# A four-layer sequence model on one core: the FP4 network rewritten as a pipeline of half batches, its quantizing of weights and inputs moved into the first attention, the second attention begun inside it

## The chip, the cores and the metric

The kernel runs on one core of one Trainium2 chip, as one launch. The metric is the device time in microseconds (us). A core has a matrix engine (PE, with its weight loads listed as PEld), a vector engine (DVE), a scalar engine (ACT), a general engine (POOL) and a queue engine that only issues transfers (SP). Each engine takes its own list of instructions strictly in order, and waits on semaphores for the others.

## The reference

The input is `x`, 8 batches of 512 tokens of width 128, fp32. Four blocks follow each other, each as `x = layernorm(x + block(x))`:

```
attention 0:  16 heads of width 8, softmax(q k^T / sqrt(8) - slope * |i-j|) v, output projection
FP4 network:  h = silu(xq @ gate_q^T) * (xq @ up_q^T);  y = hq @ down_q^T      (inner width 352)
attention 1:  16 heads of width 8, plain softmax, output projection
local block:  2 layers of local attention (8 heads of 64, window 64) and a gated network
```

The index `q` in the FP4 network is a quantization of blocks of 16 neighbours in the last dimension: the scale is max|block| / 6, each element divided by the scale is rounded to the nearest of 0, 0.5, 1, 1.5, 2, 3, 4, 6 with its sign, and multiplied by the scale again. It is applied to the input `x`, to the three weights and to the hidden `h`.

## The kernel before

The state lives in SBUF for the whole program: `xn` (the normalised activations) and `xs` (the sums), each 128 partitions x 32 token tiles x 128. `body` runs `attention(0, ...)`, clears some rows of `ks_`, then `ffn0`, `attention(1, ...)` and `ffn1`.

**attention.** A batch has 4 groups of 4 heads, and a group is a unit of 8 steps; 8 batches give 256 steps. A step (function `step`, from line 212) does for unit n the matrix products of scores `s_ps` (query rows against keys) and their row maximum `m` on DVE (L239), and for the unit two before (16 steps, `LAG`) the transposed scores `t_ps` with the maximum already folded in, and the exponentials `e` on ACT (L245). `values` multiplies `e` with `va` on PE. At fixed steps other work is hung in through the table `todo`: `shift` (transposes the maxima and sends them by a POOL transfer into a row of `q`, L257), `divide` (L282, L284), `end_o` and `end_y` at the end of a batch, and the operands of the next batch: `begin_x`, `begin_qk` (which splits q and k into two parts on POOL, L167 and L168, and writes them to DRAM), `load_qk` (which reads them back as `q` and `k`, L184) and `begin_v`. `end_y` ends in `add_and_stats` (L94 to L99 on DVE) and `layernorm` (L104, L105, L116 on POOL). PE's instructions are kept in the written order (L126, L127); the order on DVE, ACT and POOL is made when the program is built, by a scheduler that places an instruction where it expects its inputs to be ready. `p_s` holds two score tiles, `p_t` three banks, `e` thirteen tiles.

**Batch 0 of each attention** has its operands made ahead of the first step, with nothing beside them.

**ffn0.** `quantized` (L374 to L384) is ten instructions: a blockwise maximum, three small ones for the scale and its inverse on DVE, a product on POOL (L379), four on DVE (L380 to L383, the first takes the exponent bits of each element), a product on POOL (L384). The three weights are loaded and quantized at its start, turned by PE and copied by ACT. Then for each of 8 batches: `begin` quantizes the input (512 columns), `gated` turns it, does the gate and up products for 4 token tiles, `silu` and the product (L426, L427), and quantizes `h` for each half batch (704 columns); `down` turns the result, multiplies with `wd`, and adds (L94 to L99), and `layernorm` ends on ACT (L112). Nothing here is held in the written order.

Of the kernel before, what the change touches and what calls it, by code (L numbers as in the profile page):

```python
# [9 lines left out]
F32 = mybir.dt.float32  # L10
# [8 lines left out]
P = 128  # L19
B, S, D = 8, 512, 128  # L20
NT = S // P
# [19 lines left out]
def body(ctx, tc, x, consts, rows, wa0, wa1, acols, bo, wf, wqkv, wo, w1, w2, cols, b2r, qs, ks, out):  # L41
# [77 lines left out]


    def attention(li, alibi, qs_, ks_, late=None):
# [6 lines left out]
        with ExitStack() as st:  # L128
# [11 lines left out]
            qb = const.tile([P, 1], F32, name="qb")  # L140
            nc.vector.tensor_tensor(qb, col[:, 0:1], col[:, 1:2], ALU.mult)
            va = []
            for i in range(2):
                v = const.tile([P, NT, 16, 32], F32, name=f"va{i}")
                nc.gpsimd.memset(v, 0.0)
                nc.gpsimd.memset(v[:, :, :, 8:9], 1.0)
                va.append(v)


            def begin_x(b, h):  # L150
                ps = bank("xt_ps")
                for c in range(NT):
                    tr(ps[:, c * P : (c + 1) * P], xn[:, b * NT + c, :], ident)
                h["xT"] = work.tile([P, S], F32, tag="xT", name="xT", bufs=1)
                nc.scalar.copy(h["xT"], ps)

            def begin_qk(b, h, n):
                ps = bank("qk_ps")
                mm(ps, lhsT=w[:, n * P : (n + 1) * P], rhs=h["xT"], start=True, stop=True)
                t = work.tile([P, S], F32, tag=f"x{n}", name="x", bufs=1)  # L160
                if n == 0:
                    nc.scalar.activation(t, ps, AF.Identity, bias=qb, scale=col[:, 0:1])  # L162
                else:
                    nc.scalar.activation(t, ps, AF.Identity, bias=col[:, 2:3])
                parts = work.tile([P, 2, S], F32R, tag=f"hl{n}", name="parts", bufs=1)
                hi, lo = parts[:, 0, :], parts[:, 1, :]
                nc.gpsimd.tensor_copy(hi, t)  # L167
                nc.gpsimd.tensor_tensor(lo, t, hi.bitcast(F32), ALU.subtract)  # L168

                far = dram.tile([2, 2, 64, S], F32R, tag=f"far{n}", name="far")  # L170
                for j in range(2):
                    nc.sync.dma_start(
                        out=far[j].bitcast(F32).rearrange("a c t -> c a t"), in_=parts[64 * j : 64 * j + 64].bitcast(F32)
                    )
                h["far", n] = far

            def load_qk(b, h, n, part):

                dst, pp = (qs_, ks_)[n][b % 2], slice(4 * part, 4 * part + 4)
                for j in range(2):  # L180
                    both = h["far", n][j].bitcast(F32).rearrange("a (p d) t -> a d p t", d=8)
                    for r in range(4):
                        at = 64 * j + 8 * r
                        nc.sync.dma_start(  # L184
                            out=dst[at : at + 8, pp].bitcast(F32), in_=both[r // 2 if n == 0 else r % 2][:, pp]
                        )

            def begin_v(b, h):
                h["o"] = work.tile([P, NT, P], F32, tag="o", name="o", bufs=3)
                ps = bank("v_ps").rearrange("p (c d) -> p c d", c=NT)  # L190
                for c in range(NT):
                    mm(ps[:, c, :], lhsT=h["xT"][:, c * P : (c + 1) * P], rhs=w[:, W_V : W_V + P], start=True, stop=True)
                nc.scalar.copy(va[b % 2][:, :, :, 0:8], ps.rearrange("p c (h d) -> p c h d", d=8))
# [15 lines left out]
            def step(u, i, v, k):  # L209
# [30 lines left out]
                if v:  # L240
                    if alibi:
                        corrected(ts, vlo, 64, True)
                    for j in range(2):
                        e = work.tile([P, S], F32, tag="e", name="e", bufs=13)
                        nc.scalar.activation(e, ts[j], AF.Exp, scale=float(SLOPES[2 * vp + j]) if alibi else 1.0)  # L245
                        v["e"].append(e)
# [64 lines left out]
            batch, units = [{} for _ in range(B)], []  # L311
            for n in range(B * G):
# [8 lines left out]
                if g == 0 and b + 1 < B:  # L321
# [9 lines left out]
                    later(s + 20, with_bias, b + 1)  # L331
                if g == G - 1:
                    later(z + 15, end_o, batch[b])
                    later(z + 18, end_y, b, batch[b])

            begin_x(0, batch[0])
            begin_qk(0, batch[0], 0)
            begin_qk(0, batch[0], 1)
            for part in range(2):
                for j in range(2):  # L340
                    load_qk(0, batch[0], j, part)
            begin_v(0, batch[0])
# [3 lines left out]
            with_bias(0)  # L346
            if late:
                late()
            for s in range(B * G * NU + LAG + 20):
# [8 lines left out]
    def ffn0():  # L358
        with ExitStack() as st:
            pool = lambda name, bufs, **k: st.enter_context(tc.tile_pool(name=f"f{name}", bufs=bufs, **k))  # L360
            const, work = pool("c", 1), pool("w", 2)
            p_g, p_t = pool("g", 2, space=PSUM), pool("t", 4, space=PSUM)

            def quantized(src, n, tag):

                nb = n // 16
                blocks = lambda t: t.rearrange("p (n k) -> p n k", k=16)  # L370
                over = lambda t: t.unsqueeze(2).broadcast_to([P, nb, 16])
                tile_ = lambda name, w: work.tile([P, w], F32, tag=f"{name}{tag}", name=name)
                sc, inv, y, m = tile_("sc", nb), tile_("inv", nb), tile_("y", n), tile_("m", n)
                nc.vector.tensor_reduce(sc, blocks(src), AX.X, ALU.max, apply_absolute_value=True)  # L374
                nc.vector.tensor_scalar(sc, sc, float(np.float32(1.0) / np.float32(6.0)), 1e-12, ALU.mult, ALU.max)
                nc.vector.reciprocal(inv, sc)

                nc.vector.tensor_scalar_mul(inv, inv, 1.0 - 2.0**-23)
                nc.gpsimd.tensor_tensor(blocks(y), blocks(src), over(inv), ALU.mult)  # L379
                nc.vector.tensor_single_scalar(m.bitcast(I32), y.bitcast(I32), 0x7F800000, ALU.bitwise_and)  # L380
                nc.vector.tensor_scalar(m, m, 1.0, 1.5 * 2.0**22, ALU.max, ALU.mult)
                nc.vector.tensor_tensor(y, y, m, ALU.add)
                nc.vector.tensor_tensor(y, y, m, ALU.subtract)  # L383
                nc.gpsimd.tensor_tensor(blocks(y), blocks(y), over(sc), ALU.mult)  # L384
                return y


            wgu = const.tile([P, 2, NI], F32, name="wgu")
            wd = const.tile([P, 3, D], F32, name="wd")
            wraw = const.tile([P, F_ALL], F32, name="wraw")  # L390
            nc.sync.dma_start(out=wraw, in_=wf)
            for j in range(2):
                wq = quantized(wraw[:, j * 3 * P : (j + 1) * 3 * P], 3 * P, "w")
                ps = p_t.tile([P, 3 * P], F32, tag="tr", name="w_ps")
                for c in range(3):
                    nc.tensor.transpose(ps[:, c * P : (c + 1) * P], wq[:, c * P : (c + 1) * P], ident)
                nc.scalar.copy(wgu[:, j, :], ps[:, 0:NI])
            wq = quantized(wraw[:, 6 * P : F_ALL], NI, "w")
            ps = p_t.tile([P, 3, P], F32, tag="tr", name="wd_ps")
            for c, (at, n) in enumerate(I_CH):  # L400
                nc.tensor.transpose(ps[0:n, c, :], wq[:, at : at + n], ident)
            for c, (at, n) in enumerate(I_CH):
                nc.scalar.copy(wd[0:n, c, :], ps[0:n, c, :])

            def begin(b):
                return quantized(xn[:, b * NT : (b + 1) * NT, :].rearrange("p c d -> p (c d)"), S, "x")

            def gated(b, xq):
                ps = p_t.tile([P, S], F32, tag="tr", name="xq_ps")
                for c in range(NT):  # L410
                    nc.tensor.transpose(ps[:, c * P : (c + 1) * P], xq[:, c * P : (c + 1) * P], ident)
                xqT = work.tile([P, S], F32, tag="xqT", name="xqT")
                nc.scalar.copy(xqT, ps)
                hq = []
                for half in range(2):
# [15 lines left out]
            def down(b, hq):  # L431
                for half in range(2):
                    hT = work.tile([P, 3, 2, P], F32, tag="hT", name="hT")
                    for c, (at, n) in enumerate(I_CH):
                        ps = p_t.tile([P, 2, P], F32, tag="tr", name="hq_ps")
                        for t in range(2):
                            nc.tensor.transpose(ps[0:n, t, :], hq[half][:, t * NI + at : t * NI + at + n], ident)
# [478 lines left out]
```

## Time and profile before

| what | us |
|---|---|
| median of 3 runs (2046.76 to 2053.12) | 2050.5 |
| the profiled execution, its device time | 2052.7 |
| its span, first to last instruction | 2050.9 |
| first row maximum of attention 0 | 39.1 |
| last `xn` of attention 0 normalised (L116) | 535.3 |
| last `xn` of the FP4 network normalised (L112) | 723.9 |
| first row maximum of attention 1 | 746.5 |
| 17th row maximum of attention 1 (first step with exponentials) | 766.8 |

The times of the last five rows are counted from the start of the span. The page gives busy shares of the engines, in the span (PE 83%, DVE 71%, ACT 57%, POOL 40%) and in 40 slices of 51 us, with the clock that the matrix engine was granted. Attention 0 fills slices 2 to 11, the FP4 network 11 to 15, attention 1 15 to 23, the local block the rest. A row of groups reads: line, engine, operation, result<-inputs, shapes, count | busy us, mean ns of one | idle time of the engine just before, and what ended it.

### The profile page before, as it was taken

Reading aid. Unit: us, or ns where it says so; the run is one execution under the profiler, and the core shown is the slowest. Engines: PE = TensorE matmul, PEld = TensorE weight load, DVE = VectorE, ACT = ScalarE, POOL = GpSimd, SP = SyncE. Lnnn points to the kernel's source line nnn. Section 1 sums busy time; section 2 is a strip of 40 time slices with the busy share of each in tenths; the row PEclk is TensorE's granted clock in tenths of the full one; section 3 lists DMA queues with packets and bytes.
Section 4 is the critical chain, followed back from the end, with each engine's and each line's share of the span. In section 5 each row is a group of like instructions: output and inputs, shape, how many; then the busy total and the mean of one; then the engine's idle time right before and its main releaser. Section 6 shows DMA issues by size and latency. Waiting matters only on the chain.

```text
span 2050.9 us, 41924 instructions
## 1 busy us (share of the span) xinstructions
PE 1712.4 (83%) x16277; PEld 981.8 (48%) x16293; DVE 1459.0 (71%) x2612; ACT 1168.8 (57%) x2749; POOL 829.0 (40%) x880
## 2 busy tenths in 40 slices
PE   1899999999476559999999757888988888888893
PEld 0445455555254424444444324556556555656562
DVE  2677777776588648888889356777777777777752
ACT  0376777777232217877778515566665566655650
POOL 3402222213445451222221434555555555666653
PEclk6699999999787659999999869999999999999997
DMA  5722222310000033333320001111111111111110
GB/s 115 185 54 64 62 52 57 64 23 2 12 1 0 0 97 79 66 65 64 71 63 2 22 16 24 30 31 33 30 32 34 33 32 32 35 35 32 29 30 21
DMA packets 91640, 88.68 MB, mean 43 GB/s; under 512 B 45825, under 2 KB 57473, under 8 KB 91442
## 3 DMA queue, kind: packets, MB, share of 16 engines
q1 hardware_dynamic: 86752, 85.00, 19.1%
q8 instruction: 129, 2.11, 0.4%
q0 software_dynamic: 4096, 0.54, 0.2%
q14 instruction: 69, 0.57, 0.1%
q10 hardware_dynamic: 594, 0.47, 0.1%
HBM read 41.33 MB, written 18.87 MB: 29 GB/s over the span
## 4 chain that ended last, share of the span: by engine, by line
PE 23%; DVE 19%; ACT 15%; POOL 3%; issue 2%; DMA 1%; SPq 1%; ACTq 0%; POOLq 0%; DVEq 0%
ACT pw L466 8%; PE av L126 6%; PE s_ps L126 5%; DVE t L567 4%; DVE r L563 4%; DVE ss L571 3%; PE t_ps L126 3%; DVE m L627 3%; ACT sq L466 2%; PE qk_ps L464 2%; ACT e L245 1%; DVE nrm L590 1%; PE qk_ps L126 1%; DVE u L742 1%; PE p_ps L465 1%
## 5 line engine op out<-in xcount | busy, mean ns | idle before, releaser
L239 DVE TENSOR_REDUCE m<-s_ps 128x2 f32<-128x1024 f32 x512 | 624.2, 1225 | 207.1 <-PE s_ps L126 203.0
L245 ACT ACTIVATE e<-t_ps 128x512 f32<-128x512 f32 x1024 | 555.8, 595 | 185.4 <-PE t_ps L126 175.2
L126 PE MATMUL av<-e,va 128*32 128x256 f32 x4096 | 328.6, 393 | 10.4 <-ACT avs L274 10.3
L466 ACT ACTIVATE pw<-sp,m,nrm 128x128 f32<-128x128 f32 x512 | 226.5, 461 | 183.7 <-DVE m L629 183.0
L126 PE MATMUL s_ps<-k,q 63*128 63x512 f32 x1024 | 266.9, 515 | 48.3 <-DMA k<-far 24.0
L126 PE MATMUL t_ps<-q,k 64*128 64x512 f32 x1024 | 249.0, 449 | 0.0
L257 POOL DMA_DIRECT2D q<-mt x128 | 68.4, 538 | 437.7 <-ACT mt L253 437.7
L126 PEld LDWEIGHTS s_ps<-k,q 63*128 63x128 f32 x1024 | 100.3, 190 | 242.2 <-issue 153.9
L640 POOL TENSOR_TENSOR pw<-pw,den 128x1024 f32<-128x1024 f32 x64 | 121.2, 1894 | 211.3 <-DVE den L639 169.1
L574 POOL TENSOR_TENSOR r<-r,t 128x1024 f32<-128x1024 f32 x64 | 151.0, 2359 | 97.5 <-DVE t L567 95.1
L563 DVE TENSOR_TENSOR r<-qk_ps,tab 128x512 f32<-128x512 f32 x128 | 87.3, 682 | 103.0 <-ACT sq L466 103.0
L464 PE MATMUL qk_ps<-wqkv_s,hT 128*128 128x512 f32 x256 | 136.3, 659 | 16.7 <-DVE t L567 15.9
L126 PEld LDWEIGHTS t_ps<-q,k 64*128 64x128 f32 x1024 | 122.9, 189 | 20.7 <-ACT e L245 10.6
L126 PEld LDWEIGHTS av<-e,va 128*32 128x32 f32 x4096 | 81.8, 108 | 104.1 <-issue 68.8
L465 PE MATMUL p_ps<-cst,pw 128*128 128x128 f32 x512 | 76.3, 284 | 55.1 <-DVE xs L705 31.1
L466 ACT ACTIVATION_READ_ACCUMULATOR pw<-sp,m,nrm 128x1 f32 x512 | 106.1, 207 | 0.0
L126 PEld LDWEIGHTS <-sel 64*128 64x128 bf16 x2048 | 66.8, 97 | 76.4 <-issue 46.6
L467 ACT COPY v<-v_ps 128x512 f32<-128x512 f32 x64 | 37.6, 587 | 105.5 <-PE v_ps L464 105.5
L567 DVE TENSOR_TENSOR t<-qk_ps,tab 128x256 f32<-128x256 f32 x256 | 95.4, 414 | 0.0
L671 DVE COPY pT<-p_ps 128x512 f32<-128x512 f32 x128 | 84.2, 686 | 15.3 <-PE p_ps L465 14.6
L465 PEld LDWEIGHTS p_ps<-cst,pw 128*128 128x128 f32 x512 | 55.8, 142 | 72.3 <-DVE xs L705 25.3
L167 POOL CAST parts<-x 128x512 fp32r<-128x512 f32 x32 | 19.4, 607 | 170.3 <-ACT x L162 166.4
(161 smaller groups left out, 3234.3 us busy)
## 6 DMA issues: line engine op xcount, KB each, us to landing
far<-parts SPq DMA_DIRECT2D x64, 256.0 KB
q<-far SPq DMA_DIRECT2D x256, 64.0 KB
k<-far SPq DMA_DIRECT2D x256, 64.0 KB
ve<-v SPq DMA_DIRECT2D x112, 128.0 KB
xn<-in_x SPq DMA_DIRECT2D x8, 256.0 KB
q<-mt POOLq DMA_DIRECT2D x128, 4.0 KB, 2.9
hn<-xs SPq DMA_DIRECT2D x16, 128.0 KB
out<-xn SPq DMA_DIRECT2D x8, 256.0 KB
```

Source lines behind the costliest of these rows:

```text
L126: mm = lambda *a, **k: tc.keep_in_program_order(nc.tensor.matmul(*a, **k))
L239: nc.vector.tensor_reduce(u["m"][:, :, pp, blk], both, AX.X, ALU.max)
L245: nc.scalar.activation(e, ts[j], AF.Exp, scale=float(SLOPES[2 * vp + j]) if alibi else 1.0)
L257: nc.gpsimd.dma_start(out=q[at : at + 1, 2 * g : 2 * g + 2, :].bitcast(F32).rearrange("o a (c t) -> o (a c) t", t=P), in_=mt[8 * j : 8 * j ...
L464: mm = lambda *a, **k: tc.keep_in_program_order(nc.tensor.matmul(*a, **k))
L465: tr = lambda *a, **k: tc.keep_in_program_order(nc.tensor.transpose(*a, **k))
L466: act = lambda *a, **k: tc.keep_in_program_order(nc.scalar.activation(*a, **k))
L563: nc.vector.tensor_tensor(heads(r[:, n]), heads(ps[:, n]), cos.unsqueeze(1).broadcast_to([P, HEADS, DH]), ALU.mult)
L567: nc.vector.tensor_tensor(heads(t2[:, n])[:, :, a : a + 32], heads(ps[:, n])[:, :, 32 - a : 64 - a], sin[:, a : a + 32].unsqueeze(1).broad ...
L574: nc.gpsimd.tensor_tensor(r, r, t2, ALU.add)
L640: nc.gpsimd.tensor_tensor(pw.rearrange("p s r k -> p (s r) k"), pw.rearrange("p s r k -> p (s r) k"), den.rearrange("p s r -> p (s r)").un ...
L671: nc.vector.tensor_copy(h["pT"][:, s], ps)
```

## The change

1. `quantized` becomes a function of `body` with its tiles given by the caller. The exponent step changes: the bits are no longer masked on DVE; ACT takes the absolute value (`AF.Abs`), and the next DVE instruction uses other constants.
2. `first_spare` hangs into `todo` of attention 0: at steps 34, 44 and 54 a load of one weight, three steps later its quantizing, four later its turning (3 transposes on PE and the copies on ACT); and, 4 steps after `end_y` of batches 0 to 6, the quantizing of that batch's `xn` into `xs`.
3. `va` (both), `wgu`, `wd` and `qb` are now made once in the pool `ops`, after the `ks_` of that pool are cleared. `e` has 11 tiles for 13. The making of `h["o"]` moves to `hold_o`.
4. `ffn0` works on 16 half batches in a pipeline, in the written order on PE, and on DVE, ACT and POOL for its own steps. In iteration t it turns and gates half t, quantizes the hidden of half t-1, turns that of t-2, and multiplies, adds and takes the moments of t-4. Batch 7's input is quantized in iteration 5.
5. In iterations 9 to 16 `ffn0` makes the operands of batches 0 and 1 of attention 1, and loads them; attention 1 starts with two batches begun, and adds the bias to both ahead of its first step.

```diff
-            def quantized(src, n, tag):
+    def quantized(src, n, y, m, dst, small):
...
-                nc.gpsimd.tensor_tensor(blocks(y), blocks(src), over(inv), ALU.mult)
-                nc.vector.tensor_single_scalar(m.bitcast(I32), y.bitcast(I32), 0x7F800000, ALU.bitwise_and)
-                nc.vector.tensor_scalar(m, m, 1.0, 1.5 * 2.0**22, ALU.max, ALU.mult)
-                nc.vector.tensor_tensor(y, y, m, ALU.add)
-                nc.vector.tensor_tensor(y, y, m, ALU.subtract)
-                nc.gpsimd.tensor_tensor(blocks(y), blocks(y), over(sc), ALU.mult)
+        nc.gpsimd.tensor_tensor(blocks(y), blocks(src), over(inv), ALU.mult)
+        nc.scalar.activation(m, y, AF.Abs)
+        nc.vector.tensor_scalar(m, m, 1.5, 2.0**22, ALU.max, ALU.mult)
+        nc.vector.tensor_tensor(y, y, m, ALU.add)
+        nc.vector.tensor_tensor(y, y, m, ALU.subtract)
+        nc.gpsimd.tensor_tensor(blocks(dst), blocks(y), over(sc), ALU.mult)
...
+    def quantize_weights(later, at, j, temps, small, bank, tr):
...
+        later(at, load)
+        later(at + 3, lambda: quantized(h["y"], n, h["y"], h["m"], h["y"], small))
+        later(at + 7, turn)
...
-                        e = work.tile([P, S], F32, tag="e", name="e", bufs=13)
+                        e = work.tile([P, S], F32, tag="e", name="e", bufs=11)
...
-                if g == 0 and b + 1 < B:
+                if g == 0 and begun <= b + 1 < B:
...
-            with_bias(0)
+            for b in range(max(begun, 1)):
+                with_bias(b)
...
+            if spare:
+                spare(later, lambda b: (b * G + G - 1) * NU + LAG + 22, work, bank, tr)
...
-    def ffn0():
+    def ffn0(qs_, ks_, va, batch):
...
+            for t in range(N + 7):
+                at_(t, turned)
+                at_(t - 1, in_units)
+                at_(t - 4, down)
+                at_(t, gated, 0)
+                at_(t, gated, 1)
+                at_(t - 1, magnitudes)
+                at_(t, product, 0)
+                at_(t, product, 1)
+                at_(t - 4, added)
+                at_(t, largest)
+                at_(t - 1, rounded)
+                at_(t, scales)
+                at_(t - 2, turned_h)
+                at_(t - 4, moments)
+                at_(t - 1, back)
+                b, odd = divmod(t - 5, 2)
+                if 0 <= b < B:
+                    if odd:
+                        shape[b] = normed(b)
+                    elif b:
+                        normed_x(b - 1, *shape.pop(b - 1))
...
+                if t in operand:
+                    operand[t]()
...
+        def first_spare(later, done, work, bank, tr):
+            temps = lambda: [work.tile([P, S], F32, tag=t, name=t, bufs=1) for t in ("qy", "qm")]
+            for j in range(3):
+                quantize_weights(later, 34 + 10 * j, j, temps, work, bank, tr)
+            for b in range(B - 1):
+                later(done(b), lambda b=b: quantize_tokens(b, *temps(), work))
```

In the new `ffn0`, `in_units` and `back` are the two POOL products, `magnitudes` the absolute value on ACT, `rounded` the three DVE instructions between them, `scales` the three small DVE instructions, `moments` the four of the layer norm's statistics; `normed` is four small POOL instructions, `normed_x` four on ACT.

## The prediction

> **What bounds the kernel now.** I read the windows by stage first, then the groups and waits of the FP4 network, then the timelines of the places that the change touches. In the windows the columns after the stretch are its length, busy us (instructions) of PE, PEld, DVE, ACT and POOL, the granted clock, DMA share and GB/s.
>
> ```profile
> 100.00:500.00 400.00, 395.29 (x4901) 202.02 (x4900) 306.35 (x350) 282.33 (x544) 87.72 (x122) 1.00 0.25 50
> 535.30:723.90 188.60, 108.53 (x461) 78.42 (x461) 149.61 (x328) 49.13 (x126) 85.70 (x86) 0.73 0.00 1
> 723.90:746.50 22.60, 6.04 (x18) 3.29 (x18) 2.22 (x4) 2.65 (x5) 20.73 (x40) 0.65 0.41 113
> 746.50:766.80 20.30, 15.87 (x42) 6.21 (x41) 18.30 (x17) 3.59 (x5) 4.92 (x6) 0.58 0.46 108
> ```
>
> Attention 0 (first row) is bound by PE: busy 99%, full clock, DVE 77%, ACT 71%, POOL 22%. The FP4 network (second) has no full engine: DVE 79%, PE 58% at a clock of 0.73. Then 22.6 us in which nearly nothing computes: the operands of attention 1 go to DRAM and back.
>
> ```profile
> L379 POOL TENSOR_TENSOR y<-h,inv 128x704 f32<-128x704 f32 x16 | 26.2, 1639 | 42.9 <-DVE inv L378 38.6 <-DVE stats L99 2.5 <-DVE sc L375 1.9
> L384 POOL TENSOR_TENSOR y<-y,sc 128x704 f32<-128x704 f32 x16 | 23.2, 1450 | 27.3 <-DVE y L383 21.6 <-DVE stats L99 3.3 <-DVE sc L375 2.5
> POOL y L379 <- DVE inv L378: 39.2, 16, 10.4
> POOL y L384 <- DVE y L383: 36.4, 18, 3.3
> PE s_ps L126 <- DMA q<-far: 15.5, 2, 14.1
> ```
>
> DVE and POOL hand the quantizing back and forth, and wait for each other; the last row is the gap before attention 1. The end of a batch inside attention 0 (batch 1 here), DVE then POOL:
>
> ```profile
> 213.78 0.36 DVE L99 BATCH_NORM_AGGREGATE stats<-bn 128x2 f32<-128x6 f32 x4
> 214.34 1.23 DVE L239 TENSOR_REDUCE m<-s_ps 128x2 f32<-128x1024 f32 x1 [0.19 <-PE s_ps L126]
> 215.80 1.23 DVE L239 TENSOR_REDUCE m<-s_ps 128x2 f32<-128x1024 f32 x1 [0.23 <-PE s_ps L126]
> ...
> 214.24 0.24 POOL L104 TENSOR_SCALAR rstd<-stats 128x4 f32<-128x4 f32 x1 [1.96 <-DVE stats L99]
> 216.19 3.13 POOL L116 TENSOR_SCALAR xn<-xs,stats,rstd 128x128 f32<-128x128 f32 x4
> 219.30 1.27 POOL L168 TENSOR_TENSOR parts<-x,parts 128x512 fp32r<-128x512 f32 x1
> ```
>
> Call the end of the statistics E (214.1). The batch's `xn` is done at 219.3, E+5.2, beside which DVE does three or four row maxima. The plain step is 1.46 us, the mean step of a unit 1.6.
>
> **What the Trainium skill says.**
> - "SBUF — State Buffer", Who interferes with whom: a `tensor_scalar` in a two-port mode and a GpSimd instruction exclude each other for the whole instruction. The trace agrees: L380 takes 0.48 us alone and 1.21 where it meets POOL:
>
> ```profile
> 680.61 1.53 POOL L384 TENSOR_TENSOR y<-y,sc 128x704 f32<-128x704 f32 x1 [2.13 <-DVE y L383]
> 680.82 1.60 DVE L380 TENSOR_SCALAR m<-y 128x512 int32<-128x512 int32 x1
> ```
>
> - "TensorE: Matmul & The Clock Gate", Part 1: the clock is half after an idle window of about 3.4 us, full after a busy one. The trace has windows of 3.4 us and factors 0.5 and 1.0, but attention 0 stayed at half from 69.0 to 89.5 though PE was busy all through from 75.8: four windows to warm up, not one.
> - Same page, The array is 16x 32x32: ACT and DVE are strict queues. So what stands behind a waiting instruction waits too; no run here shows another order.
> - Price: "ScalarE: Activation LUTs", What ACT_TABLE_LOAD costs: 186 + 0.833 N ns, so by estimate 0.77 us for an absolute value of 704, 0.61 for 512. The trace's copy of 512 (0.59) agrees.
>
> **The change part by part.** Sum against the profiled 2052.7 us (span 2050.9 and 1.8 around it), which lies 2.2 above the median.
>
> *Start, +4.2.* `va` was cleared at 0.7 to 4.3; now it stands on POOL behind the two `ks_`, which end at 16.1. POOL's split of k and q began at 16.0 and ended at 19.7. ACT's order now puts the copy into `va` ahead of q's activation: cleared at 19.9, copy 0.6, activation 0.8, cast 0.6, two differences of 1.25: 24.4. SP was ready for `far` at 20.2 and has all later loads behind it: 24.4 - 20.2.
>
> *Weights, +18.6.* In the built order DVE takes a weight's maximum after step 41's (51's) row maximum, and PE stands at its transposes in the same step. The chain, from the rows of the weights' own groups (L374 0.50, L379 0.83, L381 to L383 1.4, L384 0.93) and the price of ACT: DVE 0.9, POOL 0.84, ACT 0.5, DVE 1.4, POOL 0.95, with hand-overs 4.9 us; before it m 1.2. PE resumes 6.4 after the row maximum began, in place of 0.85: 5.5. The step's exponentials stand on ACT behind the copy of the turned weight, 0.5 more. So 6.0 twice. The third lies together with batch 0's input: 6.6.
>
> *Tokens, +30.* For batches 1 to 4 DVE's order is E, one row maximum, then the blockwise maximum of `xn`, which is there at E+5.2. DVE waits from E+1.4 to E+5.25; the next row maximum, which could begin at E+1.65, begins at E+5.9. Two score tiles give PE about 1.0 us: it stalls 2.6 at step 94 (counting as for batch 1), 0.6 more at 95. Then ACT's order has the absolute value ahead of step 94's exponentials; the POOL product in front of it ends at E+10.5, so they run from 11.15, and the three banks hold PE: step 96 begins at E+12.85 in place of 7.45. That is 5.4 each, and kept, as PE has no slack. For batches 5 and 6 the maximum stands one row maximum later, and `xn` is there at E+4.65 (no split of q and k); ACT's wait is left: 4.2 each. 4 x 5.4 + 2 x 4.2.
>
> *Clock, +9.* Nine such stalls of 2 to 5 us may halve the clock. A half window costs 3.4 x (1 - 1.46/2.05) = 1.0; four cost 4. I take one for each stall; both ends, 0 and 36, go into the range.
>
> *`e` 11 for 13: 0.* PE writes t_ps of step s after the values of step s-1, so a tile used 11 earlier is free. Its cover is PE's written order. DMA of the weights (0.57 MB): hidden behind seven steps before their use.
>
> *FP4 network, -53.8.* Before: 723.9 - 535.3 = 188.6. After: DVE's order puts batch 7's blockwise maximum ahead of the pipeline, so it starts at 535.3 (in old time): 1.4 for that batch's scale, 2 products, maximum, scale: first `in_units` after 4.7. One interval from `in_units` to the next: POOL 1.4, ACT 0.77, DVE's three by their start-to-start times 0.45 + 0.75 + 0.85, POOL 1.4, the inverse scale behind POOL's port 0.15, hand-overs 0.3: 6.1. DVE's own sum of starts is 5.1, PE's at full clock 5.1; so the hand-over chain sets it, no engine. From iteration 6 on every second interval has `normed` between `back` and `in_units`, waiting for `moments`: 0.5 + 1.95, on average 1.2: 7.3. 15 intervals: 5 x 6.1 + 10 x 7.3 = 103.5. Batch 7 inside it (POOL 2.1, DVE 1.8): 4. Operands of attention 1 (8 ACT instructions of 0.6 to 0.8, some beside other work): 4. PE cold in the beginning: 3.6. Tail: in_units to y 5.9, turn and copies 1.8, down and add 2.4, moments, normed and ACT 4.9: 15. Sum 4.7 + 103.5 + 11.6 + 15 = 134.8, saved 53.8. Not shown by the trace: the interval with PE at half clock. PE then needs 10 us for 5.1 and holds `gated` behind `down`: 9.1 for 7.3, 27 more; at best 6.1 throughout, 18 less, and no extras, 8 less.
>
> *Start of attention 1, -22.9.* From 723.9 to the 17th row maximum took 42.9. Now the last `xn` is followed by c_ps and s_ps, 1.8 us, then 16 row maxima of 1.13: 20.0. POOL's 32 bias sums (13.2 us) now stand ahead of the first `q<-mt` transfer; they end near +16.5, the transfer lands near +20, when it is needed: 0, at worst 2. *Batch 1's products out of attention 1: -3* (v_ps 1.6 and the cold start; steps 17 to 32 took 27.3 where 22.3 is usual). Later stages only shift.
>
> Sum: 4.2 + 18.6 + 30 + 9 - 53.8 - 22.9 - 3 = -17.9. 2052.7 - 17.9 = 2034.8; less the 2.2 by which the profiled execution lies above the median, **2033**.
>
> **Rivals.**
> - *Stalls hidden* (chance 0.16). Row maxima slip under the slack, half of the 62 us lost in attention 0 is not lost, and the pipeline keeps 6.1 (18 less). For: DVE has 23% free there. Against: it stands in one queue. 2033 - 31 - 18 = 1984.
> - *Slower: the clock in attention 0* (0.2). Each stall leaves PE at half clock for several windows, as from 75.8 to 89.5. Above 3 us each, in place of my 1.0 (9 x 2 = 18), the kernel is slower than before. At 5 each it is 36 more: 2069. Against: in the local block the half windows last 3.4.
> - *The two cancel* (0.14): PE is at half clock for two thirds of the pipeline, 18 of the 27 us: 2051, within 0.3%.
> - *It doesn't do what it says*: the pipeline might have to wait for the last `xn` of attention 0, so that nothing overlaps. That is covered, as I start it there; the gap of 22.6 goes in any case.
>
> **How the numbers follow.** My forecast 2033 has 0.5 (itself 2012 to 2044). Faster: 0.5 + 0.16 = 0.66; same 0.14; slower 0.20. 0.3% (6 us) is about what a measurement of this kernel can tell from no change. The range reaches to the middle of the hidden case and of the clock case, and leaves out some 0.08 and 0.1 beyond: 1985 to 2068.
>
> **What would show it.** Right: two row maxima at each batch end of attention 0 about 5.5 us apart, three stalls of PE of 5 us at `w_ps`, attention 0 ending 50 to 62 later; the network 130 to 140 long with POOL's products each 6 to 8 us; no wait for `q<-far` before attention 1. Wrong: attention 0 no longer than before (stalls hidden), or a clock below 0.95 in it, or a network over 155 us with PE full.

## The result, and the profile after

The changed kernel takes 2057.8 us (median of 10 runs, 2051.6 to 2066.5), the kernel before 2049.6 in the same series (10 runs, 2046.8 to 2053.5): a ratio of 1.0041, 95% interval 1.0025 to 1.0057. So it is slower by 0.4%, where I had forecast 2033: inside the stated range (1985 to 2068), but on the other side of the kernel before. The profiled execution has a span of 2056.0 (before: 2050.9). The profile of one experiment (the early loads) was taken from a disturbed execution with a mean clock of 0.80, so only the times of its undisturbed runs and the order of its instructions are used.

The windows by stage of the changed kernel, with the columns as before (PE, PEld, DVE, ACT, POOL, clock, DMA share, GB/s):

```profile
100.00:560.00 460.00, 423.76 (x4853) 210.45 (x4849) 324.63 (x409) 285.42 (x552) 104.10 (x139) 0.91 0.21 44
604.50:748.64 144.14, 102.42 (x478) 73.29 (x478) 106.99 (x231) 63.02 (x138) 69.65 (x75) 0.86 0.15 33
748.64:768.94 20.30, 14.33 (x37) 5.57 (x37) 18.55 (x19) 1.54 (x2) 14.34 (x34) 0.50 0.45 74
```

Attention 0, where PE was 99% busy at full clock, is now at 92% and a clock of 0.91; its last `xn` comes at 604.5 instead of 535.3. The network takes 144.1 instead of 188.6. The gap of 22.6 behind it is gone: attention 1's 17th row maximum comes 20.3 after the last `xn` of the network. So 69.2 is lost, 44.5 and 22.6 are won, and 3 us more go in attention 1 and after: 5.1 in the span. Row maximum n below is the one of step n.

Batch 1's end in attention 0, DVE first, then POOL, then ACT:

```profile
239.47 0.36 DVE L99 BATCH_NORM_AGGREGATE stats<-bn 128x2 f32<-128x6 f32 x4
240.10 1.23 DVE L294 TENSOR_REDUCE m<-s_ps 128x2 f32<-128x1024 f32 x1 [0.27 <-PE s_ps L229]
245.05 0.69 DVE L129 TENSOR_REDUCE sc<-xn 128x32 f32<-128x512 f32 x1 [3.72 <-POOL xn L116]
...
241.88 3.13 POOL L116 TENSOR_SCALAR xn<-xs,stats,rstd 128x128 f32<-128x128 f32 x4
248.92 1.06 POOL L134 TENSOR_TENSOR qy<-xn,inv 128x512 f32<-128x512 f32 x1 [2.67 <-DVE inv L133]
...
244.04 1.08 ACT L300 ACTIVATE e<-t_ps 128x512 f32<-128x512 f32 x2 [0.96 <-PE t_ps L229]
250.01 0.63 ACT L135 ACTIVATE qm<-qy 128x512 f32<-128x512 f32 x1 [4.88 <-POOL qy L134]
250.54 1.07 ACT L300 ACTIVATE e<-t_ps 128x512 f32<-128x512 f32 x2
```

Read the square brackets: DVE stands 3.72 us at the blockwise maximum until POOL has `xn`, with row maxima behind it; ACT stands 4.88 at the absolute value until POOL has the product, with exponentials behind it. Both waits are where the prediction put them. The first weight, DVE and then PE:

```profile
122.99 0.54 DVE L129 TENSOR_REDUCE sc<-qy 128x24 f32<-128x384 f32 x1
126.25 0.36 DVE L136 TENSOR_SCALAR qm<-qm 128x384 f32<-128x384 f32 x1 [1.96 <-ACT qm L135]
...
128.91 0.90 PE L230 MATMUL w_ps<-cst,qy 128*128 128x128 f32 x3 [5.94 <-POOL qy L139]
```

The maximum at 122.99 waits for nothing: the weight's load was issued at 103.5, 19.5 us earlier. It stands behind row maximum 41 because the order was built so. PE is by then at the transposes of the same weight and waits 5.94 us for the whole chain.

The products of POOL in the network, the answer to the two group rows shown of before:

```profile
L423 POOL TENSOR_TENSOR y<-y,sc 128x704 f32<-128x704 f32 x16 | 22.6, 1410 | 45.8 <-DVE sc L423 42.4 <-DVE y L423 3.4
L423 POOL TENSOR_TENSOR y<-h,inv 128x704 f32<-128x704 f32 x16 | 22.1, 1384 | 9.3 <-PE gp L423 8.1 <-DVE inv L423 0.7 <-DMA q<-far 0.2
```

The wait ahead of `y<-h,inv` fell from 42.9 to 9.3 us (8.1 of it at the start of the network), that ahead of `y<-y,sc` rose from 27.3 to 45.8: POOL now idles inside the quantizing of one half batch instead of between two.

### The profile page after: what moved, and what is told of

Its sections match the earlier page's. It is cut to its first block, busy times and chain, and to the rows that moved or that the text cites. A ratio compares the mean times of both kernels' runs of the same rounds, so it can differ in the third digit from the quotient of the medians.

```text
span 2056.0 us, 41914 instructions
## 1 busy us (share of the span) xinstructions
PE 1738.7 (85%) x16277; PEld 984.7 (48%) x16293; DVE 1437.3 (70%) x2584; ACT 1184.1 (58%) x2768; POOL 821.2 (40%) x876
## 4 chain that ended last, share of the span: by engine, by line
PE 24%; DVE 21%; ACT 15%; POOL 5%; issue 3%; DMA 1%; SPq 0%; POOLq 0%; ACTq 0%; DVEq 0%
ACT pw L589 8%; PE av L229 7%; PE s_ps L229 5%; DVE t L690 4%; DVE r L686 4%; DVE ss L694 3%; DVE m L750 3%; PE t_ps L229 3%; ACT sq L589 2%; PE qk_ps L587 2%; POOL y L423 1%; ACT e L300 1%; DVE u L865 1%; DVE nrm L713 1%; PE p_ps L588 1%
## 5 line engine op out<-in xcount | busy, mean ns | idle before, releaser
L229 PE MATMUL av<-e,va 128*32 128x256 f32 x4096 | 339.7, 405 | 9.9 <-ACT avs L329 9.8
L229 PE MATMUL s_ps<-k,q 63*128 63x512 f32 x1024 | 274.8, 529 | 42.1 <-DMA k<-far 23.9
L229 PE MATMUL t_ps<-q,k 64*128 64x512 f32 x1024 | 260.2, 463 | 11.1 <-ACT e L300 4.7
L763 POOL TENSOR_TENSOR pw<-pw,den 128x1024 f32<-128x1024 f32 x64 | 121.2, 1894 | 211.5 <-DVE den L762 183.6
L587 PE MATMUL qk_ps<-wqkv_s,hT 128*128 128x512 f32 x256 | 140.7, 678 | 16.3 <-DVE t L690 15.5
L229 PEld LDWEIGHTS <-sel 64*128 64x128 bf16 x2048 | 69.2, 101 | 84.2 <-issue 53.3
L589 ACT ACTIVATE sq<-qk_ps 128x1024 f32<-128x1024 f32 x64 | 68.4, 1069 | 34.5 <-PE qk_ps L587 34.3
```

The lines of the kernel that those rows point to most:

```text
L229: mm = lambda *a, **k: tc.keep_in_program_order(nc.tensor.matmul(*a, **k))
L587: mm = lambda *a, **k: tc.keep_in_program_order(nc.tensor.matmul(*a, **k))
L589: act = lambda *a, **k: tc.keep_in_program_order(nc.scalar.activation(*a, **k))
L763: nc.gpsimd.tensor_tensor(pw.rearrange("p s r k -> p (s r) k"), pw.rearrange("p s r k -> p (s r) k"), den.rearrange("p s r -> p (s r)").un ...
```

## The experiments

Theory Q: what attention 0 loses is waiting at the heads of strict queues, set by where the instructions stand, plus the half clock behind each stall (a half window is one stretch of 3.4 us at half clock). Its rival A: the added work itself, on DVE, ACT and POOL and at the port that DVE and POOL share. For the network, theory H: POOL's products form a chain of hand-overs. Its rival P: PE at half clock sets the intervals. All ratios are to the kernel before, run beside them.

### Weights loaded earlier, and not quantized at all

```diff
-            h["y"], h["m"] = (t[:, 0:n] for t in temps())
+            h["y"] = tokens(B - 1 - j)[:, 0:n]
...
-        later(at, load)
-        later(at + 3, lambda: quantized(h["y"], n, h["y"], h["m"], h["y"], small))
+        later(at - 30, load)
+        later(at + 3, lambda: quantized(h["y"], n, h["y"], temps()[1][:, 0:n], h["y"], small))
```

> Edit: the changed kernel with the three weights loaded 30 steps earlier, into rows of xs that are not yet used; all their other instructions stay, and nothing is left out. In the built order DVE then takes the three maxima after row maxima 19, 34 and 54, with row maxima in between the rest, instead of all seven instructions right behind row maximum 41 (51, 63). Theory Q (the loss is waiting at the heads of strict queues, set by position, plus the half clock behind each stall): the 26.9 us lost at the three weights nearly all return, 2057.8 - 24 = 2034 (2030 to 2038), the same as without the weights' quantizing. Rival A (the loss is the added work itself, on DVE, ACT and POOL and at their shared port): the work is all still there, so at most 5 us return, 2053 or more.

The other kernel of this pair only drops the line with `quantized`:

> Edit: the changed kernel without the quantizing of the three weights (left out of the computation: the weights are loaded and turned, but stay unquantized). Both theories: the 26.9 us of steps 40 to 64 return, 2031 (2028 to 2036). What it tells is by comparison with the early loads: under Q the two are within 4 us, under A 20 apart.

Measured: early loads 2045.4, ratio 0.9964 (0.9950 to 0.9978); no quantizing of weights 2043.5, 0.9959 (0.9948 to 0.9971). The two are 2 us apart, within their intervals: the work costs next to nothing once it stands elsewhere, as Q has it. (The row maxima ahead of the weights are 19, 31 and 48; the text on record counted the last two wrongly.) Both regained 12 to 14 us by the medians and 16 to 17 by the ratios, so both miss the 24 to 27 on record. The profile of the kernel without quantizing, which is 7 us under that kernel's median, shows the reason for part of it: at step 80 it is 6.4 behind the kernel before, instead of 25.8, because batch 0's tokens now stall PE on their own, for 7.5 us; in the changed kernel that stall lay inside the third weight's.

### Tokens in stages, and not quantized at all

The ten instructions are held in the written order, one stage to a step (shortened; the names in the tuple stand for the stages, `scale` for three instructions and `nothing` for an empty step):

```diff
-                later(done(b), lambda b=b: quantize_tokens(b, *temps(), work))
+                later(done(b) + 4, lambda b=b: in_stages(later, done(b) + 5, ...))
...
+        for i, f in enumerate((largest, scale, product, nothing, absolute, clip, add, subtract, back)):
+            later(at + i, f)
```

> Edit: the changed kernel with the ten instructions of each token batch (0 to 6) held in written order at steps of their own, beginning 9 steps after end_y instead of 4: maximum, scales, POOL product, absolute value, the three of the rounding, POOL product, one stage in each step. Nothing is left out. Theory Q: no engine's queue has anything at its head that is not ready, so the 42 us of six token batches (7.85 x 4 + 6.4 + 5.7 = 43.5) return but for about 1 us of port contention a batch: 2057.8 - 37 = 2021 (2014 to 2028). Rival A: at most a quarter of it returns, 2047 or more.

> Edit: the changed kernel without the quantizing of the inputs of batches 0 to 6 (left out of the computation: the network takes these inputs unquantized). Both theories: 43.5 us return, 2014 (2008 to 2020). By comparison with the staged tokens: under Q at most 8 us between them, under A 25 or more.

Measured: staged 2010.9, ratio 0.9801 (0.9778 to 0.9824); without 2015.9, 0.9818 (0.9793 to 0.9844). Both have attention 0 end at 561, 43 us earlier than the changed kernel, and what is left (26.1 and 25.6 us at step 80) is the weights'. The staged kernel is 10 us faster than its number on record: the 1 us of port contention that I allowed for each batch does not show either. So seven batches' quantizing costs nothing there that these runs can tell if no instruction comes to the head of its queue before its input is ready. Rival A is out for the tokens.

### Everything in stages

Weights too are staged, loaded 32 steps ahead; in the second kernel weights 1 and 2 stand 4 and 8 steps earlier: `(34, 78, 110)` becomes `(34, 74, 106)`.

> Edit: the changed kernel with the token batches in stages as in the run of staged tokens, and the weights too: loaded 32 steps ahead into unused rows of xs, quantized in written order with a step for each stage, beginning at steps 38, 82 and 114, turned 11 steps after that. Nothing is left out. Theory Q (waits at queue heads): all of attention 0's loss is gone; the run of staged tokens lost 25.8 us at the weights alone in its profile, so 2010.9 - 24 = 1987 (1982 to 1993), attention 0 ending within 2 us of the kernel before (535.3). Rival A (the added work): 2002 or more.

> Edit: the run of all stages, with the second and third weight 4 and 8 steps earlier (stages from steps 78 and 110, turned at 89 and 121), so that their last POOL product comes ahead of the end of a batch and no longer stands on POOL behind the layer norm's four products. In the run of all stages the two lost 6.1 and 5.0 us, PE waiting 3.6 at w_ps for that product. Theory Q (heads of queues): both losses go, 1996.6 - 11 = 1986 (1982 to 1990), and attention 0 ends within 2 us of the kernel before. Rival A (the added work): 1994 or more.

Measured: 1996.6, ratio 0.9740 (0.9723 to 0.9757), and 1988.0, 0.9686 (0.9661 to 0.9710). The first missed its number by 10 us, and A would have had 2002 or more. POOL and PE of that kernel show what was left:

```profile
218.40 1.25 POOL L221 TENSOR_TENSOR parts<-x,parts 128x512 fp32r<-128x512 f32 x1
219.63 0.83 POOL L162 TENSOR_TENSOR xs<-xs,sc 128x384 f32<-128x384 f32 x1
...
220.51 0.90 PE L256 MATMUL w_ps<-cst,xs 128*128 128x128 f32 x3 [3.08 <-POOL xs L162]
```

The weight's last product (L162) was ready, as its input was done on DVE at 210.3, but it stood on POOL behind the layer norm and `parts` of batch 1's end, and PE waited for it (3.08 us, not the 3.6 of the text on record): the same kind of stall on another queue. Moved out of that place, it is gone, and so is the one of weight 2. Attention 0 then ends at 535.8, against 535.3 before, with all the quantizing in it (535.8 to 536.6 in the three kernels that share this part), so A is out for the weights too. Its window and a token batch, DVE then ACT:

```profile
130.00:530.00 400.00, 391.77 (x4789) 200.66 (x4786) 304.79 (x398) 285.15 (x553) 115.09 (x148) 1.00 0.20 45
```

```profile
227.07 1.23 DVE L320 TENSOR_REDUCE m<-s_ps 128x2 f32<-128x1024 f32 x1 [0.36 <-PE s_ps L255]
228.21 0.68 DVE L154 TENSOR_REDUCE sc<-xn 128x32 f32<-128x512 f32 x1
228.83 1.23 DVE L320 TENSOR_REDUCE m<-s_ps 128x2 f32<-128x1024 f32 x1
...
235.22 0.63 ACT L158 ACTIVATE qm<-qy 128x512 f32<-128x512 f32 x1
```

PE is back at 98% and full clock. DVE takes the blockwise maximum between two row maxima, and neither that maximum nor ACT's absolute value has a wait in brackets.

### Which of the two token waits costs what

From the kernel just told, the maximum, scales and first product are put back where the changed kernel has them; the absolute value and what follows stay in stages. So only DVE's wait for `xn` is left.

```diff
-                later(done(b) + 4, lambda b=b: in_stages(later, done(b) + 5, ...))
+                later(done(b), lambda b=b: in_two(later, done(b) + 7, ...))
```

> Edit: the run with the weights in the clear, but of each token batch the maximum, the scales and the POOL product stand where the changed kernel has them (the maximum two row maxima behind the statistics, so that DVE waits for xn), and only the absolute value, the rounding and the last product come later, in stages from 7 steps on. Nothing is left out. It splits the token stall of 6.1 us plus 1.8 at half clock. My prediction's working: DVE's wait alone stalls PE 2.6 and 0.6 us in batches 1 to 4 (in batches 5 and 6 nothing), ACT's wait the rest; with the half clock behind it 4 x (3.2 + 1.8) = 20, attention 0 ending at 556, time 2008 (2002 to 2014). Rival C: DVE's slip is hidden behind the score tiles and ACT's queue is the whole stall: at most 1 us a batch, 542 or less, 1993 or less. Rival D: DVE's wait is the whole stall: 6 to 8 in each of batches 1 to 4, 560 or more, 2012 or more.

Measured: 2015.3, ratio 0.9839 (0.9807 to 0.9870); attention 0 ends at 561.6, 25.9 later than with everything in stages. DVE at the end of batch 1:

```profile
222.99 0.69 DVE L172 TENSOR_REDUCE sc<-xn 128x32 f32<-128x512 f32 x1 [3.74 <-POOL xn L116]
223.59 1.22 DVE L341 TENSOR_REDUCE m<-s_ps 128x2 f32<-128x1024 f32 x1
```

By the row maxima of the two kernels the wait costs 4.4 us in each of batches 1 to 3 (my working: 3.2 and 1.8 of clock), but also 4.3 in batch 0 and 2.9, 3.3 and 3.0 in batches 4 to 6. Of the 43.4 us that batches 1 to 6 lose in the changed kernel, 22.3 are DVE's wait; the rest goes with the later stages, of which ACT's wait is the visible one (no run has it alone). C is out. The totals lie on D's side, but not for D's reason: no batch costs 6 to 8, and three batches that D and I had left out (0, 5 and 6) add 10.6. So DVE's wait is about half of it. The clock's part can be read here too: batches 1 to 3 each have one half window behind the wait, batch 4 has the same wait (3.73 us) and none, and costs 1.5 less. My text was wrong in that DVE stands in batches 5 and 6 too (2.33 and 2.40 us in the changed kernel's trace), where I had put nothing.

### The network: normed moved, PE given more work, the operands taken out

```diff
                 at_(t - 1, in_units)
+                if t >= 7 and t % 2 == 1 and (t - 7) // 2 < B:
+                    shape[(t - 7) // 2] = normed((t - 7) // 2)
...
                 at_(t - 1, back)
-                        shape[b] = normed(b)
```

> Edit: the run of all stages, and in the network the four POOL instructions of normed moved from behind back to behind the next in_units; nothing is left out. Theory H (POOL's products are a chain of hand-overs, and normed lies in it): seven intervals lose 1.9 us each, 13 us less than the run of all stages (10 to 16), the network some 131 long for 144. Rival P (PE at half clock sets the intervals): at most 4 us less.

Measured: 2005.4, ratio 0.9769 (0.9744 to 0.9793), 9 us more than its base (1996.6), where 10 to 16 less was expected. Part of the 9 is not the network: attention 0, the same program in both, ends 4.7 later in this profile. The network itself took 147.4 for 143.7; but the unchanged network took 141.2 to 147.1 in six profiles (of the changed kernel, no quantizing of weights, the staged tokens, everything in stages, the weights moved, DVE's wait alone), so of this one only the missing gain is shown. Two intervals, from one first POOL product to the next, became shorter (8.14 to 6.34, 9.69 to 6.87), the ones with operands longer. POOL there:

```profile
659.69 1.39 POOL L449 TENSOR_TENSOR y<-h,inv 128x704 f32<-128x704 f32 x1 [0.18 <-DVE inv L449]
668.67 0.68 POOL L220 CAST parts<-x 128x512 fp32r<-128x512 f32 x1 [7.60 <-ACT x L215]
669.43 1.79 POOL L221 TENSOR_TENSOR parts<-x,parts 128x512 fp32r<-128x512 f32 x1
671.18 1.38 POOL L449 TENSOR_TENSOR y<-y,sc 128x704 f32<-128x704 f32 x1
```

The norm's four instructions left the place where they cost 1.9 us, but two of them took 0.94 and 0.91 us at the new place (0.20 and 0.23 in the base), ACT's four normalisations now came later, and with them ACT's `x`, for which POOL's cast stands 7.60 us (4.05 in the base) with `back` behind it. One head of a queue was traded for another.

For the next, the inner four transposes of `turned_h` stand in `for _ in range(2):`.

> Edit: the run of all stages, and in each of the network's 16 half batches the four large transposes of turned_h done twice, which leaves the result as it is and adds 0.44 us of PE work at full clock. Rival P (PE at half clock sets the network's intervals): a busier PE stays at full clock more, 8 us or more less than the run of all stages. Theory H (the chain of hand-overs sets them): within 3 us of it, or up to 7 us more (16 x 0.44).

Measured: 1999.0, ratio 0.9746 (0.9731 to 0.9760); network 142.3 for 143.7, clock 0.91 for 0.88. PE was busier, and the time did not fall as P had it (8 us or more). But the clock rose by only 0.03, so P's number is missed, while what the half clock costs in the network is not measured by this.

The next leaves out the table `operand`, its loads and `batch += h`, from the kernel with everything in stages and the weights moved.

> Edit: the run before it in this list, without the operands of attention 1 in the network; attention 1 makes them ahead of its first step, as the kernel before did. Nothing is left out. My prediction priced these operands at 4 us within the network. Theory O (they stand at the heads of ACT's and POOL's queues and cost more): the network's intervals from the 9th on fall to 6.4 and 8.1 by turns, 11 us less, some 132 long. Rival P (half clock and DVE set these intervals): at most 5 less. In both the start of attention 1 takes 20 to 23 us more, so 1986 - 11 + 22 = 1997 under O, 2003 or more under P.

Measured: 2009.1, ratio 0.9790 (0.9774 to 0.9807). The network took 143.1 for 142.3. Two intervals with operands fell from 8.4 to 6.4, but others rose (10.1 to 10.9, 8.2 to 10.4). So O is out: the operands, which I had priced at 4, cost nothing there that the scatter of the network lets show. The number that P had here, for half clock and DVE together, 2003 or more, was met. The start of attention 1 went back to 42.6 from 20.3. That part of the change is worth what I wrote.

### The network's chain broken

```diff
+            turned(0, half_[0])
             for t in range(N + 7):
-                at_(t, turned)
                 at_(t - 1, in_units)
-                at_(t - 4, down)
+                at_(t - 2, back)
+                normed, as above
...
                 at_(t - 1, magnitudes)
+                at_(t + 1, turned)
+                at_(t - 4, down)
...
+                at_(t, largest)
+                at_(t, scales)
                 at_(t - 4, added)
-                at_(t, largest)
                 at_(t - 1, rounded)
-                at_(t, scales)
...
-                at_(t - 1, back)
```

> Edit: the run of all stages, and in the network's written order: back one iteration later, behind the next in_units, with normed behind it; scales ahead of rounded and added; the next half's turned behind this half's gated. Nothing is left out. Theory H: no POOL product waits for the rounding of the same half any more, so the interval falls to the sum of DVE's starts, 5.1 to 6.2: 8 + 15 x 5.8 + 18 = 113 for the network instead of 144, 31 us less than the run of all stages (20 to 36). Rival P (PE at half clock sets the intervals): at most 10 less. Rival N (DVE with its port waits sets them, about 8 in iterations with much POOL work): 10 to 18 less.

> Edit: the weights in the clear as in the first run of this list, and the network's written order changed: back one iteration later behind the next in_units, normed behind it, the next half's turned behind this half's gated, scales ahead of added, moments and rounded, and attention 1's operand steps ahead of turned_h. Nothing is left out. Theory Q (waits at queue heads): intervals of 6.1 to 6.5 throughout, network 8 + 3 + 14 x 6.3 + 4 + 17 = 120, so 1986 - 24 = 1962 (1955 to 1968). Rival N (DVE's sum with its waits for the port POOL holds, 7.2 as in the run with the chain broken): network 133, 1975 (1970 to 1980).

Measured: 1993.1, ratio 0.9717 (0.9702 to 0.9731), and 1975.3, 0.9635 (0.9616 to 0.9654). The first is only 3.5 us under its base: it misses H (20 to 36) and N (10 to 18) and stays in what P allowed (at most 10). It took 139.9 for its network: intervals of 6.0 to 7.2 for the most part, but 10.3 and 11.2 where POOL's cast waited 2.3 to 2.7 us for a late ACT. In the second the operand steps come ahead of `turned_h`, and the weights are moved: 130.3 for 142.3 with the weights moved alone, with plain intervals of 5.7 to 6.6, 7.2 to 7.5 with either `normed` or the operands on POOL, and 9.2 with both. Q's 1962 is missed and N's 1975 is met. The network's window, DVE over one interval with operands, and POOL beside it:

```profile
536.63:666.89 130.26, 91.82 (x478) 68.78 (x478) 111.67 (x231) 63.46 (x138) 69.94 (x75) 0.92 0.16 37
...
604.54 1.57 DVE L449 TENSOR_SCALAR m<-m 128x704 f32<-128x704 f32 x1
606.22 1.82 DVE L449 TENSOR_TENSOR y<-y,m 128x704 f32<-128x704 f32 x2
607.96 0.95 DVE L449 TENSOR_TENSOR h<-up,si 128x352 f32<-128x352 f32 x2
609.01 0.89 DVE L449 TENSOR_REDUCE sc<-h 128x44 f32<-128x704 f32 x1
609.93 0.19 DVE L449 TENSOR_SCALAR sc<-sc 128x44 f32<-128x44 f32 x1
610.15 0.43 DVE L449 RECIPROCAL inv<-sc 128x44 f32<-128x44 f32 x1
610.61 0.84 DVE L449 TENSOR_SCALAR inv<-inv 128x44 f32<-128x44 f32 x1
...
604.35 1.38 POOL L449 TENSOR_TENSOR y<-h,inv 128x704 f32<-128x704 f32 x1
610.14 1.27 POOL L221 TENSOR_TENSOR parts<-x,parts 128x512 fp32r<-128x512 f32 x1
```

There is no bracket and no gap on DVE: here it is the bound now; over the whole network it is busy for 86% (75% with the weights moved alone). The first DVE row takes 1.57 us beside POOL's product at 604.35 (0.52 in the changed kernel at 666.50, where POOL is idle), the last 0.84 beside POOL's `parts` (0.19 at 617.88). The Trainium skill's "SBUF — State Buffer", Who interferes with whom, has a `tensor_scalar` in a two-port mode and a GpSimd instruction block each other for the whole instruction; these durations agree, and what the two rows take more is 1.7 us of the interval. This version is 3.7% under the kernel before and 4.0% under the changed one (1975.3 to 2057.8).

## Why the prediction was wrong, step by step

All are us in the profiled executions, changed kernel against before, each rounded; the first four make up the 69.2 of attention 0.

| step of the prediction | predicted | measured |
|---|---|---|
| start | +4.2 | -1.1 |
| weights (third with batch 0's input), clock included | +21.6 | +26.9 |
| tokens, batches 1 to 4, clock included | +25.6 | +31.3 |
| tokens, batches 5 and 6, clock included | +10.4 | +12.1 |
| network | -53.8 | -44.5 |
| start of attention 1 | -22.9 | -22.6 |
| batch 1's products out of attention 1 | -3 | +2.0 |
| the rest of attention 1 and later | 0 | +0.9 |
| sum | -17.9 | +5.1 |

- **Start: wrong, in the other direction.** POOL cleared `va` from 16.0 to 19.5, as said. But ACT's copy into `va`, with q's activation behind it, waited only for the first of the two (17.8), not for both, so `far` was issued at 22.2 instead of 24.4, 1.9 later than before; and its reads caught up, for the first row maximum came at 38.6 in place of 39.1. The profiles of the kernels with the same start lie between 1.8 earlier and 0.6 later at step 24, so what is shown is that the 4.2 did not come.
- **Weights and tokens: the mechanism was right, the size was off.** The positions, the engines and the waiting instructions were those named. Behind the three weights the next row maximum came 7.2, 6.8 and 7.5 late, for 6.0, 6.0 and 6.6, and the steps at half clock behind it cost 3.0, 1.0 and 1.3. At the end of batch 1 row maximum 96 came 6.0 late, not 5.4, and the steps at half clock behind it cost 1.8, not 1.0. As the clock was at half from 247.8, ahead of that row maximum at 254.0, a part of the 6.0 is the clock's as well; the runs don't tell how much. The *Clock* step is the term of attention 0 that failed, twice over. I took one half window for each stall, and the trace has 10.2 us at half clock (three windows) for five of the six token batches, 13.7 for the first weight and 6.8 for the others. And I priced a window at 1.0, while 3.0 us in the 7.8 from row maximum 42 to the end of the half clock behind the first weight make 1.3 for each window, and batch 4 of the kernel with DVE's wait alone gives 1.5. The rival "the clock in attention 0" had its mechanism right. Whether its threshold, 3 us for each stall, was reached behind the token batches stays open; the sign turned because the network fell short as well.
- **`e` with 11 tiles: right.** With 11 tiles and everything in stages attention 0 ends 0.5 later than with 13.
- **Network: half right.** The start took 8.1: ACT's table load (1.28 us at 604.9) and four gate and up products at half clock, 604.96 to 609.87, stand in it. The sum had 4.7 and, apart, 3.6 for a cold PE, so this was right in size, though it did not name the table load; the tail was right too, 14.8 for 15. So the whole shortfall lies in the 15 intervals: 121.2 for 111.5 (103.5, and 4 each for batch 7 and the operands). The plain interval was 6.34 to 6.68 for 6.1. The others were up to 11.5, and in the kernel without operands those with `normed` are 10.4 to 10.9 from the eighth on, for 8.55 in my sum (6.1, 0.5 and 1.95). The term that failed is this one: it had POOL's four `normed` instructions and left ACT's four normalisations at nothing. This is read from the trace; no run has them alone. The one interval that has `normed` ahead of ACT's first normalisations took 8.1. ACT, POOL and PE of an interval of 10.4:

```profile
658.54 1.65 ACT L423 ACTIVATE xn<-xs,mr,rstd 128x128 f32<-128x128 f32 x4
660.09 0.35 ACT L423 COPY xqT<-xq_ps 128x256 f32<-128x256 f32 x1
664.18 0.46 ACT L423 ACTIVATE si<-gp 128x352 f32<-128x352 f32 x1 [1.88 <-PE gp L423]
664.54 0.78 ACT L423 ACTIVATE m<-y 128x704 f32<-128x704 f32 x1
...
669.08 1.38 POOL L423 TENSOR_TENSOR y<-y,sc 128x704 f32<-128x704 f32 x1 [5.59 <-DVE sc L423]
670.86 1.04 POOL L423 TENSOR_TENSOR rstd<-rstd,half 128x4 f32<-128x4 f32 x1
...
660.50 1.30 PE L423 MATMUL gp<-wgu,xqT 128*128 128x352 f32 x2 [3.15 <-ACT xqT L423]
```

  The four normalisations stand ahead of the copy `xqT`; PE waits 3.15 for it, its products come late and at half clock, the silu that waits for them stands ahead of the absolute value, and POOL waits 5.59 for its second product. That the operands cost 4 is not borne out by the kernel without them; that the intervals are set by waits between queues and not by a full engine is borne out by the best order, until DVE is full. Two sums of mine were also wrong: 6.1 throughout is 12 less than 103.5, not 18, and 9.1 throughout is 33 more, not 27. And the 0.48 and 1.21 us that I gave for L380 mix shapes: with 704 columns it takes 0.51 to 0.53 alone and 1.11 to 1.69 where it meets POOL for most of its time.
- **Start of attention 1: right**, and the kernel without operands shows what it is worth (42.6 against 20.3).
- **Batch 1's products out of attention 1: not to be told from the clock.** Steps 272 to 288 have the same program in all kernels with two batches begun, and took from 25.7 to 30.7 us in their profiles, in which the clock is at half for 30.7 to 37.6 us around the start.

So no single step turned the sign. Attention 0 cost 7.4 us more than predicted (the clock and the length of the stalls, 12.7 together, against a start that was 5.3 better); the network gave 9.3 less, by the trace through ACT's part in the intervals and the half clock behind it; batch 1 gave 5 less. What the experiments add is that the cost of attention 0 was not one of the work: it was 69 us of waiting and of half clock behind it, of which a different order leaves 0.5. What stays open: of the 26.9 us at the weights 7.5 remain as batch 0's own stall, and the other 19.4 came back in full in the profile, but only as 14 in the medians and 17 in the ratios. And runs of one kernel scatter by 2 to 15 us, with and without stalls in attention 0 (11 us with everything in stages and the weights moved), so the clock's share of a single stall is known from one profile alone.

## What to carry to other kernels

Work that was hung into a stage bound by one engine was free here only where each of its instructions came to the head of its queue after its input was ready; ten dependent instructions over three engines want a step each, and an order built from expected times must be read to see whether they got it. Cost a stall with the clock behind it, and check every queue that the moved instruction stands in, since moving it away from one wait can put it ahead of another. When the waits are gone, ask which engine is full: here DVE, with its waits for POOL's port.

## What the runs showed of the hardware that was not expected

PE's clock fell without PE being idle for a whole window. With DVE's wait alone, two windows of 3.4 us in which PE was busy 2.17 and 2.13 us are followed by one at half clock; PE's idle time in the two is mainly one gap of 2.43 us across the boundary:

```profile
220.27:223.68 3.41, 2.17 (x30) 0.85 (x28) 0.69 (x2) 1.81 (x4) 3.41 (x5) 1.00 0.00 0
223.68:227.10 3.42, 2.13 (x26) 1.07 (x28) 3.42 (x8) 1.01 (x2) 0.75 (x2) 1.00 0.47 107
227.10:230.51 3.41, 3.41 (x32) 1.54 (x30) 2.44 (x3) 1.17 (x3) 0.82 (x1) 0.50 0.38 99
```

It is no fixed threshold of the busy time, as far as these windows show: in batch 4 of the same run PE was busy 1.93 and 2.37 us in two such windows (404.58 to 411.40, counted in steps of 3.41 from the change of the clock at 353.38; one gap of 2.41), and the clock stayed full.

In the changed kernel two windows with PE busy throughout stayed at half behind the first weight before the clock came back:

```profile
131.72:135.14 3.42, 3.42 (x30) 1.30 (x22) 1.44 (x2) 2.40 (x5) 0.00 (x0) 0.50 0.01 5
135.14:138.55 3.41, 3.41 (x26) 1.56 (x26) 1.77 (x3) 1.10 (x3) 0.00 (x0) 0.50 0.02 5
138.55:141.96 3.41, 3.41 (x52) 1.73 (x48) 2.45 (x2) 1.99 (x4) 0.00 (x0) 1.00 0.00 0
```

The Trainium skill's "TensorE: Matmul & The Clock Gate", Part 1, gives one idle window for the fall and one busy one for the return; here a gap of 2.43 us was enough at that place, and the return took two windows (four in the kernel before, from 75.8 to 89.5). (Ends of matmuls are modelled in the trace, so the busy shares are approximate.)
